# Gathering relation rows ahead of time: fewer groups in the first pass, more in the later layers, two tiles a bucket gathered on the spot

## The chip, the cores and the metric

The kernel runs on one core of one Trainium2 chip. The metric is the device time of one execution in microseconds (us); lower is better. The core has these engines, each with an instruction queue of its own that is worked off in order: PE (TensorE, matrix products), DVE (VectorE), ACT (ScalarE), POOL (GpSimd) and SP (SyncE, which here issues most of the transfers). Sixteen DMA engines move the data for all of them.

## The reference, cut to what matters

Four blocks follow each other over 3125 nodes of 256 features, and 103125 edges. Each adds its result to the nodes.

```python
x = x + _L0_gnn_ref(_layernorm(x), edge_index, ...)     # three graph layers
x = x + _L0_ffn_ref(_layernorm(x)[None], ...)[0]        # mixture of 16 experts, top 2
x = x + _L1_gnn_ref(_layernorm(x), edge_index, edge_type_500, ...)   # Clifford layer
x = x + _L1_ffn_ref(_layernorm(x)[None], ...)[0]        # mixture of 8 experts, top 2
```

The graph layers average the neighbours of each node (`segment_sum(h[src], dst) / deg`), multiply by two weight matrices, normalise, and add. The Clifford layer needs, for every edge, the source node's row times a row that belongs to the edge's relation, one of 500:

```python
h_src = h_hc[src]
r_uv = r_hc[edge_type]
m = clifford_linear(h_src * r_uv, msg_w, msg_b)
gate = sigmoid(r_uv.reshape(r_uv.shape[0], -1) @ gate_w.T + gate_b)
m = m * gate[:, :, None]                  # and times a norm by the degrees
h_agg = segment_sum(m, dst, num_segments=num_nodes)
h_out = clifford_linear(h_hc + h_agg, upd_w, upd_b)
```

Here only the rows of relations matter: 500 rows of 256 features and the gate, 257 numbers (`W`), multiplied by the gate beforehand and stored in the DRAM table `r_rows`.

## The kernel before, in words

The nodes are tiled into 25 buckets of 128 (`NB`, `P`). The edges of one target bucket are sorted in the first pass into 26 main tiles of 128 edges (`NS`, by source bucket) and 9 spill tiles (`SP`) for what doesn't fit.

**Stages.** (1) *First pass*: for each bucket `load` fetches windows of the edge list (`win`, SP), `rank` and `permute` place each edge in its tile (mostly DVE, with PE for counting), `lay` writes the tile's relation numbers to `main_t` and its sources to `main_s`, `build` makes the count matrix `cell` of the bucket and stores it in `cells`, and `sums_of` and `finish` compute the first graph layer. Four iterations overlap: bucket i is ranked while i-1 is permuted, i-2 is built and i-3 is summed. (2) *Layer 2* and (3) *layer 3*: `spread` prepares the rows of all buckets, then for each bucket the `cell` block is loaded again (SP, L834, four buffers, issued two iterations ahead), PE sums 75 products into `z`, and `finish` updates the nodes. In layer 2 DVE also reduces each `cell` block to degrees (`some_src`, L852) and works out the places of the spilled edges (`places`); in layer 3 the spill tiles are packed (`pack`) and the experts chosen (`choose`). (4) *The first mixture of experts* (`moe`): a routing part, then 34 tiles of 256 tokens whose rows POOL gathers (`xt`, L249, eight buffers) and whose results it scatters with addition (`f_total`, L1148). (5) *The Clifford buckets*: for every main tile PE picks the source rows with one-hot matrices (`hg_ps`, L1402), DVE multiplies them by the relation rows (`prod`, L1405), and PE sums by target with a second one-hot (`ps`, L1414). For spill tiles POOL gathers both factors itself (`hg`, `rg`, L249, six buffers each). (6) The second mixture of experts.

**Relation rows.** Main tiles don't gather their relation rows in the Clifford stage. They are gathered ahead, in groups of three tiles (`RG`): `fetch_relations(n, after)` takes the next n groups. For each it writes the relation numbers to `paced` with a small DVE operation (L296) that also reads the tile `after`, which ties the group to that point of the program; POOL then gathers three times 128 rows (L300) into `rel_rows` (four buffers). The store of a group to its DRAM tile `r_seq` (SP, L311) is issued when the next group is fetched. In the Clifford stage `relation(m)` loads two groups at a time back from `r_seq` (SP, L1376). Before the change the 650 main tiles make 217 groups that run across bucket borders.

**Who fetches.** In the first pass there are four calls of one group an iteration: at the end of `rank`, after `lay`, before `build` and after `finish`. In layer 2 `places` and `finish` call for one each; in layer 3 `choose` and `finish`. Ten more are asked for ahead of the first mixture of experts, and the rest after it. The order within each engine's queue isn't the program's: a scheduler orders the instructions of all stages by their dependences and its own idea of the times. By its order, all groups that were left stood on POOL ahead of the first token gather, or just after it.

**Order on SP.** In layers 2 and 3 the loads of `cell` blocks and the stores of `r_seq` are in one queue, two stores ahead of most loads. On DVE the reduction of block k (L852) stands ahead of the two fetches of bucket k-3. In the first pass one iteration's order on SP is three stores of groups, the store of a `cell` block, two window loads, one more store of a group, and the store of `main_s`.

Of the kernel before, what the change touches and what calls it, by code (L numbers as in the profile page):

```python
# [40 lines left out]
I32 = mybir.dt.int32  # L41
# [7 lines left out]
P = 128  # L49
N = 3125  # L50
NB = 25
# [11 lines left out]
NS = NB + 1  # L63
SP = 9
# [15 lines left out]
def gnn_moe_kernel(  # L80
# [177 lines left out]
    NM = NB * NS  # L258
    of_group = [range(t, min(t + RG, NM)) for t in range(0, NM, RG)]
# [24 lines left out]
    paced = rel_ctx.enter_context(tc.tile_pool(name="paced", bufs=1)).tile([P, NM], I32, name="paced")  # L284
# [37 lines left out]
    with ExitStack() as block:  # L322
# [65 lines left out]
        with ExitStack() as first:  # L388
# [256 lines left out]
            for i in range(NB + 3):  # L645
# [3 lines left out]
                if 0 <= i - 1 < NB:  # L649
                    moved[i - 1] = permute(i - 1, loaded.pop(i - 1), *ranked.pop(i - 1))  # L650
                    lay(i - 1, moved[i - 1])
                    if i > 1:
                        fetch_relations(1, words_of(moved[i - 1]))
# [4 lines left out]
                if 0 <= i - 3 < NB:  # L658
                    z = sums_of(i - 3, built.pop(i - 3), 0, psum)
                    done = finish(i - 3, z, 0)  # L660
                    if i > 3:
                        fetch_relations(1, done.bitcast(I32))
# [88 lines left out]
        with ExitStack() as later:  # L751
# [96 lines left out]
            for b, cell in enumerate(ahead_of(load_cell, 2)):  # L848
# [6 lines left out]
                fetch_relations(1, done.bitcast(I32))  # L855
# [19 lines left out]
            for b, cell in enumerate(ahead_of(load_cell, 2)):  # L875
# [5 lines left out]
                fetch_relations(1, done.bitcast(I32))  # L881
# [310 lines left out]
    with ExitStack() as block:  # L1192
# [107 lines left out]
        with ExitStack() as run:  # L1300
# [47 lines left out]
            DG = 7  # L1348
# [22 lines left out]
            def relation(m):  # L1371
                if m % (RC * RG) == 0:
                    held[0] = work.tile([P, RC, RG, W], F32, name="rg_seq", bufs=4)
                    first_g = m // RG
                    for i, g in enumerate(of_group[first_g:first_g + RC]):
                        nc.sync.dma_start(  # L1376
                            held[0][:, i, :len(g), :].rearrange("p r w -> p (r w)"),
                            r_seq[first_g + i])
                return held[0][:, m // RG % RC, m % RG, :]

            def summands():


                for b in range(NB):
                    s_oh = picks(b)

                    order = sorted([((t + 0.5) / NS, 0, t) for t in range(NS)] +
                                   [((t + 0.4) / SP, 1, t) for t in range(SP)])
                    d_oh = {}
                    for n, (_, spilled, t) in enumerate(order):  # L1390
                        ids = spill_d[:, b, :] if spilled else main_d[:, b, :]
                        if t % DG == 0:
                            d_oh[spilled] = drops(ids[:, t:min(t + DG, ids.shape[1])])
# [4 lines left out]
                        else:  # L1398
# [5 lines left out]
                            rg = relation(b * NS + t)  # L1404
                        nc.vector.tensor_mul(prod, hg, rg)  # L1405
                        yield (b, prod, d_oh[spilled][:, t % DG, :], n == 0,
# [74 lines left out]
```

## Time and profile before

| | |
|---|---|
| median of 3 runs | 3085.66 us (3076.42 to 3097.18) |
| the profiled execution | 3081.72 us, its span 3079.8 us |
| busy share of the span | PE 81%, weight load 64%, DVE 57%, ACT 14%, POOL 51% |
| granted PE clock, mean | 0.91 |
| relation gathers (L300) | 650, 761.3 us busy, 1.171 us each |
| first pass (130 to 706 us) | DVE 441.5 us busy, PE 404.4, POOL 381.0 |
| sums of layer 2 (771 to 1031 us) | PE 221.6 us busy, POOL 135.4, DVE 127.1 |
| sums of layer 3 (1087 to 1347 us) | PE 242.7 us busy, POOL 168.8, DVE 164.9 |
| Clifford buckets (1836 to 2565 us) | PE 700.6 us busy, DVE 577.9, POOL 466.3 |

The stage borders are read from the instructions in order of time. A busy time is that of an engine's instructions alone: the instruction that issues a transfer is short, the transfer itself is not in it. "A <- B" in a list of waits means that A stood still until B was done. The profiled execution's own time is its span and 1.9 us around it.

### The profile page before, as it was taken

To read this page: it belongs to the slowest core of one execution; us is meant where nothing else is said; L and a number is where in the kernel's file an instruction comes from. 1 tells how busy PE (TensorE), PEld (TensorE's weight loads), DVE (VectorE), ACT (ScalarE), POOL (GpSimd) and SP (SyncE) were. 2 spreads that over 40 slices of the span, in tenths; PEclk is the share of its full clock that TensorE was granted. 3 is DMA by queue.
4 is the path that set the end of the run, shared out by engine and by line. 5 is a ranking of instruction groups with operands and counts; after the bars stand their busy time and mean duration, and the time that the engine had idled before them with its cause. 6 is when DMAs were issued, how large, how long until landed. Compare 5 with 4: busy or idle time off the path is not lost.

```text
span 3079.8 us, 47955 instructions
## 1 busy us (share of the span) xinstructions
PE 2499.6 (81%) x17712; PEld 1986.2 (64%) x17712; DVE 1767.9 (57%) x4734; ACT 434.1 (14%) x1119; POOL 1566.1 (51%) x1379
## 2 busy tenths in 40 slices
PE   1767766778888999942999518999999996899997
PEld 0356654654777588832788406777777775788886
DVE  6688886766455366662233377788888787111110
ACT  1321221223000210000111050000000000122221
POOL 1067776761455256675566316666666660333331
PEclk9888897789999999976999859999999997899998
DMA  7046665652666368865777537777777770665653
GB/s 222 3 143 190 182 185 175 185 187 81 203 220 226 123 217 276 265 192 159 207 200 194 118 136 261 241 244 248 249 249 251 240 221 19 220 184 175 187 172 96
DMA packets 294160, 581.12 MB, mean 189 GB/s; under 512 B 77946, under 2 KB 176955, under 8 KB 289939
## 3 DMA queue, kind: packets, MB, share of 16 engines
q1 hardware_dynamic: 207459, 389.64, 36.9%
q0 software_dynamic: 76992, 177.86, 23.3%
q10 hardware_dynamic: 9456, 10.36, 1.1%
q8 instruction: 146, 2.39, 0.3%
q14 instruction: 107, 0.88, 0.1%
HBM read 433.05 MB, written 151.13 MB: 190 GB/s over the span
## 4 chain that ended last, share of the span: by engine, by line
PE 59%; DVE 15%; issue 7%; DMA 6%; another core or an unknown queue 5%; POOL 4%; ACT 1%; SPq 1%; POOLq 0%; DVEq 0%; ACTq 0%
PE ps L1414 12%; PE ph L1125 10%; PE py L1143 10%; PE hg_ps L1402 7%; PE z L362 5%; PE g L344 4%; POOL rel_rows L300 4%; PE z L359 2%; DVE oh_end L507 2%; DVE upto L539 2%; DMA cell<-cells 1%; PE pq L1043 1%; DMA rel_rows<-r_rows,paced 1%; DVE oh_slot L507 1%
## 5 line engine op out<-in xcount | busy, mean ns | idle before, releaser
L300 POOL DMA_INDIRECT rel_rows<-r_rows,paced x650 | 761.3, 1171 | 678.8 <-issue 158.6
L362 PE MATMUL z<-part_hi,cell 128*128 128x256 bf16 x3750 | 691.0, 285 | 23.9 <-issue 23.3
L359 PE MATMUL z<-part_lo,cell 128*128 128x256 bf16 (+1 forms) x1875 | 534.8, 285 | 18.4 <-issue 12.4
L1414 PE MATMUL ps<-prod,d_oh 128*128 128x257 f32 x1750 | 521.1, 392 | 26.5 <-issue 12.6
L362 PEld LDWEIGHTS <-cell 128*128 128x128 bf16 x3750 | 374.9, 102 | 85.0 <-issue 31.2
L1402 PE MATMUL hg_ps<-hc_part,s_oh 128*128 128x257 bf16 x1950 | 328.5, 275 | 98.0 <-DMA rg_seq<-r_seq 98.0
L1148 POOL DMA_INDIRECT f_total<-y,tok_s x126 | 198.3, 1574 | 354.0 <-DVE y L1146 275.3
L249 POOL DMA_INDIRECT hg<-hc_rows,spill_s x225 | 235.0, 1045 | 263.0 <-issue 125.9
L1143 PE MATMUL py<-w_t,hid 128*128 128x256 f32 x1472 | 335.1, 382 | 3.4 <-ACT hid L1134 3.4
L1125 PE MATMUL ph<-xT,w_t 128*128 128x256 f32 x1472 | 336.9, 386 | 0.8
L1405 DVE TENSOR_TENSOR prod<-hg_ps,rg_seq 128x257 f32<-128x257 f32 x650 | 270.4, 421 | 108.2 <-PE hg_ps L1402 65.2
L1414 PEld LDWEIGHTS ps<-prod,d_oh 128*128 128x128 f32 x1750 | 275.2, 191 | 81.5 <-issue 31.3
L1402 PEld LDWEIGHTS <-s_oh 128*128 128x128 bf16 x1950 | 191.6, 99 | 195.7 <-DVE s_oh L1358 98.4
L1146 DVE TENSOR_SCALAR y<-py,wt_q 128x256 f32<-128x256 f32 x126 | 61.0, 484 | 445.5 <-PE py L1143 440.8
L1125 PEld LDWEIGHTS ph<-xT,w_t 128*128 128x128 f32 x1472 | 280.4, 193 | 44.4 <-DVE xT L1115 3.7
L1143 PEld LDWEIGHTS py<-w_t,hid 128*128 128x128 f32 x1472 | 274.1, 191 | 50.8 <-ACT hid L1134 3.8
L249 POOL DMA_INDIRECT rg<-r_rows,spill_t x225 | 235.3, 1046 | 68.6 <-issue 68.6
L359 PEld LDWEIGHTS <-cell 128*128 128x128 bf16 x1875 | 192.5, 103 | 56.5 <-issue 23.1
L1134 ACT ACTIVATE hid<-ph,b_t 128x256 f32<-128x256 f32 x300 | 129.7, 471 | 647.8 <-PE ph L1125 524.8
L249 POOL DMA_INDIRECT xt<-f_x,tok_g x126 | 123.9, 983 | 99.0 <-DVE wt_q L1055 44.7
L507 DVE TENSOR_TENSOR oh_end<-held,iota 128x1024 bf16<-128x1024 f16 (+3 forms) x150 | 150.4, 1017 | 9.4 <-remote 5.0
L344 PE MATMUL g<-ww,hT 128*128 128x512 f32 x300 | 145.3, 629 | 8.2 <-ACT hT L143 8.0
(296 smaller groups left out, 2783.6 us busy)
## 6 DMA issues: line engine op xcount, KB each, us to landing
r_seq<-rel_rows SPq DMA_DIRECT2D x216, 385.5 KB
rg_seq<-r_seq SPq DMA_DIRECT2D x216, 385.5 KB
w_t<-in_L_ffn_W_dram SPq DMA_DIRECT2D x58, 1024.0 KB
cell<-cells SPq DMA_DIRECT2D x50, 800.0 KB
w_t<-in_L_ffn_w_dram SPq DMA_DIRECT2D x68, 512.0 KB
s_row<-main_s SPq DMA_DIRECT2D x25, 832.0 KB
cells<-cell SPq DMA_DIRECT2D x25, 800.0 KB
rel_rows<-r_rows,paced POOLq DMA_INDIRECT x650
```

The costliest lines, as they stand in the source:

```text
L249: nc.gpsimd.indirect_dma_start(out=rows, out_offset=None, in_=table, in_offset=bass.IndirectOffsetOnAxis(ap=ids, axis=0))
L300: nc.gpsimd.indirect_dma_start(out=rows[:, j, :], out_offset=None, in_=r_rows, in_offset=bass.IndirectOffsetOnAxis(ap=types[:, j:j + 1], a ...
L344: nc.tensor.matmul(g, hT[:, k, :], ww[:, layer, k, :], start=k == 0, stop=k == KD - 1)
L359: nc.tensor.matmul(z[:, :width], cell[:, sh, :], part_lo[:, sh, :width], start=sh == 0, stop=False)
L362: nc.tensor.matmul(z[:, :D], cell[:, sh, :], part_hi[:, sh, i, :], start=False, stop=sh == NB - 1 and i == 1)
L507: nc.vector.tensor_tensor(oh[:, :n, :, :], ids[:, :, None, :].to_broadcast([P, n, width, 2]), table[:, None, :width, :].to_broadcast([P, n ...
L1125: nc.tensor.matmul(ph[:, j - j0, :], w1_t[:, 0, k, j * P:(j + 1) * P], xT[:, k, :], start=k == 0, stop=k == KD - 1)
L1143: nc.tensor.matmul(py, hid[:, j, of], w2_t[:, 0, j, :], start=False, stop=j == nj - 1)
L1148: st = nc.gpsimd.indirect_dma_start(out=total, in_=y, in_offset=None, out_offset=bass.IndirectOffsetOnAxis(ap=tok_s[:, q:q + 1], axis=0), ...
L1402: nc.tensor.matmul(hg, s_oh[:, t, :], part[:, sh, i, :W], start=i == 2, stop=i == 0)
L1405: nc.vector.tensor_mul(prod, hg, rg)
L1414: nc.tensor.matmul(ps[b], d_oh, prod, start=is_first, stop=is_last)
```

## The change

It changes how many groups there are and where they are fetched. (1) The groups no longer cross bucket borders: 8 groups of three cover main tiles 0 to 23 of each bucket (`NK`), 200 groups in all. Main tiles 24 and 25 of a bucket are gathered in the Clifford stage from `r_rows`, by POOL, through the same six `rg` buffers as the spill tiles. (2) In the first pass two of the four calls are dropped: the one after `lay` and the one after `finish`. (3) In layers 2 and 3 the call after `finish` asks for two groups in odd buckets instead of one. (4) In a Clifford bucket the order of the 35 products is new: the 11 tiles that are gathered (9 spill, 2 main) are spread evenly among the 24 that are loaded. The one-hot tiles for the targets hold up to 8 columns instead of 7 for main tiles, and 5 and 4 for spill tiles.

```diff
-    NM = NB * NS
-    of_group = [range(t, min(t + RG, NM)) for t in range(0, NM, RG)]
+    NK = (NS - 2) // RG
+    of_group = [range(t, t + RG) for b in range(NB) for t in range(b * NS, b * NS + NK * RG, RG)]
...
                     lay(i - 1, moved[i - 1])
-                    if i > 1:
-                        fetch_relations(1, words_of(moved[i - 1]))
...
-                    done = finish(i - 3, z, 0)
-                    if i > 3:
-                        fetch_relations(1, done.bitcast(I32))
+                    finish(i - 3, z, 0)
...
                 done = finish(b, z, 1)
-                fetch_relations(1, done.bitcast(I32))
+                fetch_relations(1 + b % 2, done.bitcast(I32))
...
                 done = finish(b, z, 2)
-                fetch_relations(1, done.bitcast(I32))
+                fetch_relations(1 + b % 2, done.bitcast(I32))
...
-            DG = 7
+            DG = 8
...
-            def relation(m):
-                if m % (RC * RG) == 0:
+            def relation(b, t):
+                if t >= NK * RG:
+                    return gather(work, r_rows, W, main_t[:, b * NS + t:b * NS + t + 1], "rg", 6)
+                if t % (RC * RG) == 0:
                     held[0] = work.tile([P, RC, RG, W], F32, name="rg_seq", bufs=4)
...
-                    order = sorted([((t + 0.5) / NS, 0, t) for t in range(NS)] +
-                                   [((t + 0.4) / SP, 1, t) for t in range(SP)])
+                    loaded = NK * RG
+                    gathered = [(1, t) for t in range(SP)]
+                    for t in range(loaded, NS):
+                        gathered.insert((t - loaded + 1) * SP // (NS - loaded + 1) + t - loaded,
+                                        (0, t))
+                    order = sorted(
+                        [((t + 0.5) / loaded, 0, t) for t in range(loaded)] +
+                        [((i + 0.4) / len(gathered), *g) for i, g in enumerate(gathered)])
...
-                        if t % DG == 0:
-                            d_oh[spilled] = drops(ids[:, t:min(t + DG, ids.shape[1])])
+                        n_of = (DG, (SP + 1) // 2)[spilled]
+                        key = spilled, t // n_of
+                        if key not in d_oh:
+                            at = t // n_of * n_of
+                            d_oh[key] = drops(ids[:, at:min(at + n_of, ids.shape[1])])
```

More of the change, by code (lines that the diff above doesn't have):

```diff
@@ L283, in gnn_moe_kernel @@
     rel_ctx = ctx.enter_context(ExitStack())
-    paced = rel_ctx.enter_context(tc.tile_pool(name="paced", bufs=1)).tile([P, NM], I32, name="paced")
+    paced = rel_ctx.enter_context(tc.tile_pool(name="paced", bufs=1)).tile(
+        [P, NB * NS], I32, name="paced")
     stage = rel_ctx.enter_context(tc.tile_pool(name="rel_stage", bufs=4))
@@ L1369, in drops @@
                 return d_oh
-            def relation(m):
-                if m % (RC * RG) == 0:
+            def relation(b, t):
+                if t >= NK * RG:
+                    return gather(work, r_rows, W, main_t[:, b * NS + t:b * NS + t + 1], "rg", 6)
+                if t % (RC * RG) == 0:
                     held[0] = work.tile([P, RC, RG, W], F32, name="rg_seq", bufs=4)
[L1374 to L1379, printed above, removed]
+                    for i in range(RC):
+                        nc.sync.dma_start(held[0][:, i, :, :].rearrange("p r w -> p (r w)"),
+                                          r_seq[b * NK + t // RG + i])
+                return held[0][:, t // RG % RC, t % RG, :]
             def summands():
@@ L1403, in summands @@
                                                  start=i == 2, stop=i == 0)
-                            rg = relation(b * NS + t)
+                            rg = relation(b, t)
                         nc.vector.tensor_mul(prod, hg, rg)
-                        yield (b, prod, d_oh[spilled][:, t % DG, :], n == 0,
+                        yield (b, prod, d_oh[key][:, t % n_of, :], n == 0,
                                n == len(order) - 1)
```

## The prediction, made before the changed kernel had run

> **What bounds the kernel now.** I read the stage table first (busy time of each engine in stretches cut at the stage borders), then the waits of each stage, then the chain of waits inside one stage, then single instructions in order of time. The relation gathers (POOL L300, 650 of them, three to a group) run beside four stages, so each stage has to be judged by itself.
>
> Stretches: first pass, layer 2 sums, layer 3 sums, the gap before the first MoE, that MoE, the Clifford buckets. Columns: stretch, length, then busy time (and count) of PE, weight load, DVE, ACT, POOL, and the granted clock, the DMA share, GB/s.
>
> ```profile
> 130.00:706.00 576.00, 404.43 (x4953) 325.84 (x4952) 441.50 (x975) 111.66 (x278) 381.03 (x285) 0.84 0.57 169
> ...
> 771.00:1031.00 260.00, 221.55 (x1866) 183.51 (x1865) 127.05 (x323) 1.20 (x4) 135.40 (x143) 0.92 0.68 220
> ...
> 1087.00:1347.00 260.00, 242.72 (x2622) 208.42 (x2620) 164.91 (x691) 18.99 (x54) 168.77 (x151) 0.99 0.79 254
> ...
> 1421.00:1473.00 52.00, 8.29 (x24) 5.84 (x24) 0.76 (x2) 0.00 (x0) 35.09 (x37) 0.57 0.79 225
> 1473.00:1721.00 248.00, 246.67 (x1187) 208.86 (x1188) 82.95 (x190) 30.35 (x64) 151.32 (x118) 0.99 0.78 198
> ...
> 1836.00:2565.00 729.00, 700.61 (x4138) 533.31 (x4138) 577.87 (x1457) 40.37 (x121) 466.31 (x448) 0.98 0.74 240
> ```
>
> The reader is to see: DVE leads in the first pass (77%), no engine is full in layer 2 (PE 85%), PE sets layer 3 (93%), the MoE (99%) and the Clifford stage (96%). Between 1421 and 1473 nobody computes: the first expert tile waits for its token rows, which stand behind relation gathers on POOL.
>
> In layer 2 the waits of DVE name the transfer that nobody is supposed to wait for, and the chain between 925 and 960 us shows the ring behind it:
>
> ```profile
> DVE some_src L852 <- DMA cell<-cells: 77.6, 18, 9.8
> ```
>
> ```profile
> 925.27 4.41 DMA cell<-cells
> 929.67 1.72 issue
> 931.39 3.49 DVE some_src L852
> ...
> 942.96 3.63 DMA rel_rows<-r_rows,paced
> 947.15 4.89 DMA cell<-cells
> 952.93 3.49 DVE some_src L852
> ```
>
> Load of a cell block, DVE's reduction of it (in order ahead of the two fetches of the bucket three back), six gathers, their landing, the stores on SP, and only then the load of the block two further on: 947.15 - 925.27 = 21.9 us for two buckets. PE alone needs 221.6/25 = 8.9 us a bucket.
>
> **What the Trainium skill says.** "Perfetto Trace Analysis", Summary: the profiler window per engine type: the window of a POOL-issued DMA ends with its descriptors, the movement is hidden. The trace agrees: 0.95 us on POOL, but 3.63 us from the last gather's start to its landing. "SBUF — State Buffer", SBUF: two separate sides: while DVE runs certain two-port operations, POOL can't write descriptors. The trace agrees in its pattern: gathers last 0.943 to 3.072 us, mean 381.03/285 = 1.34 in the first pass, 0.95 in layer 2 and 1.13 in layer 3. "TensorE: Matmul & The Clock Gate", Part 1: an idle window of some 3.4 us halves the clock; here the clock is 0.84, 0.92 and 0.99 in the three passes, in the order of PE's idleness.
>
> **The change part by part.**
>
> *Where the groups go.* Before: 217 groups (95 in the first pass, 50 in layer 2, 50 in layer 3, 22 after). After: 25 buckets x 8 groups = 200 of which the first pass takes 23 + 24 = 47, layers 2 and 3 take 25 + 25 + 12 = 62 each, leaving 29. In the compiled order of POOL the stretch before the first token gathers holds 70 relation gathers in both kernels, and 23 more fall among the first expert tiles in the changed one.
>
> *First pass, what goes.* 48 groups, that is 144 gathers x (1.34 + 0.30 us between two) = 236 us of POOL, 48 stores on SP and 48 small DVE operations. It is tempting to book the 236 us; but the chain of the pass touches POOL and its transfers once only (444 to 465 us), and DVE is the one to ask. (1) 48 DVE operations at about 0.08 us from start to start: 4 us. (2) DVE waits for the window loads, which sit on SP behind stores that wait for gathers: 10.6 us in four waits, 4.5 us in one more at 185.75: 15 us. (3) The end of the pass: a branch waits for the last gathers, 701.3 to 706.8 us in the chain; the last group is now fetched a bucket earlier: 4 us. (4) Longer bubbles with PE and ACT (5.67, 5.84, 12.17, 3.87, 6.74, 4.95 us): sum 39, cause not visible in the trace; a few may come from a PE gone cold, since 490 to 500 us shows a clock of 0.5. Bounds 0 and 39; I take 10. Sum: -33 us, with -20 and -65 as ends. What is late next is DVE itself: quiet buckets already pass at 20.6 us with only some 3 us of waiting.
>
> *Layer 2, what is added.* Every odd bucket fetches three groups instead of two. In the compiled order of SP the load of an even-numbered block (from the eighth on) stands behind all three stores of the odd bucket that used to have two, and the reduction still stands ahead of the fetches on DVE. So the ring gains three gathers: 3 x (0.95 + 0.30) = 3.75 us. The other ring, of the odd blocks, is as before, but both go through the same in-order DVE and POOL, so the slower sets the pace: 21.6 + 3.75 = 25.4 us for two buckets, POOL being busy 15 x 1.25 = 18.8 of them. Nine turns of the ring: +34 us. Ends: +26 (a turn or two hidden) and +50 (PE, now idle up to 36% of the time, goes cold as in the first pass).
>
> *Layer 3.* Here the loads have room: block 24 is gated by the fetch of bucket 19, four buckets earlier, in both orders. PE's 10.3 us a bucket stay. But POOL needs 15 x (1.13 + 0.30) = 21.4 us for two buckets of 20.6: it falls behind by 0.8 us each time, some 10 us at the end. It used to wait there for its releasers by 27.9 + 22.9 us, which the 36 new gathers (51 us) eat. The lag costs nothing in the layer; it is paid in the gap before the MoE, where 70 gathers, and on SP 34 loads of expert numbers, stand in a row as before. +8 us (0 to 15). DMA share goes from 0.79 to about 0.9 by bytes; the four-buckets' room hides it.
>
> *First MoE.* 23 gathers x 1.25 = 29 us of POOL, ahead of some scatters. Token rows for five and a half tiles are gathered first and a tile takes 248/34 = 7.3 us; counting POOL's queue through, the rows of the seventh tile are gathered 42 us after the start and needed at 51. +1 us (0 to 8).
>
> *Clifford buckets.* 50 gathers more: POOL's mean there is 1.045 us, so 20 x 1.345 = 26.9 us of a bucket's 29.2, six buffers ahead. PE's work is the same, the one-hot tiles hold the same columns in the same six operations a bucket (8, 8, 8, 2 and 5, 4 for 7, 7, 7, 5 and 7, 2), and 17 fewer loads on SP. 0 us (-5 to +12).
>
> *Sum.* -33 + 34 + 8 + 1 + 0 = +10 us against this execution's 3081.7 (its span of 3079.8 and 1.9 around it): 3092. The median of the runs shown, 3085.7, stands 4 us above the profiled one, so this is between 3092 and 3096 against it; I give 3092. It is no difference: a measurement of this kernel tells about 1% (31 us) from none.
>
> **The rivals.**
> *Slower: POOL falls behind in layer 3.* If odd buckets catch DVE's long operations as the first pass does, a gather costs 1.34 + 0.30 = 1.64 us, 15 of them 24.6 us against 20.6, 4 us lost each pair, some 45 at the end of the layer, all of it paid in the gap before the MoE: 3092 - 8 + 45 = 3129. It decides from a mean pitch of 20.6/15 = 1.37 us on. For it: 1.43 today. Against: POOL waited 51 us in the layer and only part of DVE's work blocks it.
> *Faster: the first pass was paced by POOL after all.* Buckets that passed at 17.4, 18.5 and 19.0 us exist (from one scan L539 to the next); if the mean fell from 22.4 to 19, the pass gives 25 x 3.4 + 4 = 89 instead of 33: 3092 - 56 = 3036. For it: POOL's 12 gathers a bucket take 12 x 1.64 = 19.7 of 22.4 us. Against: DVE is busy 17 us a bucket and its short waits on PE recur without any transfer.
> *The ring of layer 2 doesn't stretch,* since something else already fills those 3.75 us: 3092 - 34 = 3058, just short of a gain that could be told. Against: the chain from gather to load has no slack in it.
>
> **How the numbers follow.** Forecast, within its own 3055 to 3116: 0.43, with the third rival inside it. POOL behind in layer 3, or a colder PE in layer 2 with it: 0.30. First pass paced by POOL: 0.27. So faster by over 1% 0.27, within 1% 0.43, slower by over 1% 0.30. Range 3033 to 3132: to the two outer rivals, with a tenth left beyond each.
>
> **What would show it.** Right: layer 2's cell loads come in pairs 25 us apart (21.9 now), DVE's wait for them grows by some 35 us, the first pass shortens by 20 to 65 us with DVE at 80% or more, POOL waits for almost nothing in layer 3, and the gap before the MoE is 50 to 65 us. Wrong: a pair pitch under 23 us, a first pass shorter by over 70 us, a gap over 75 us, or PE idle in the Clifford stage for token or relation rows.

## The result, and the profile after

The changed kernel takes 3201.25 us (median of 4 runs, 3182.09 to 3215.37) against 3084.05 us for the kernel before (4 runs beside it): ratio 1.037, 95% interval 1.0295 to 1.0448. It is slower; the forecast was 3092 us. The profiled execution took 3213.51 us, its span is 3211.6.

The stretches of the changed kernel, cut where the same stage begins and ends in it: first pass, layer 2, layer 3 (from its first product, so its counterpart of before is 302 us, not the 260 us that begin after the last block of the spread), first mixture, Clifford buckets. Columns as ahead: stretch, length, busy time (and count) of PE, weight load, DVE, ACT, POOL, granted clock, DMA share, GB/s.

```profile
129.00:585.00 456.00, 358.86 (x4961) 295.51 (x4959) 433.34 (x932) 107.12 (x279) 240.75 (x144) 0.95 0.45 133
644.00:969.00 325.00, 247.70 (x1873) 191.58 (x1871) 130.31 (x339) 1.58 (x5) 169.94 (x180) 0.82 0.66 204
978.00:1342.00 364.00, 318.92 (x2768) 237.34 (x2766) 187.21 (x740) 40.35 (x117) 196.12 (x179) 0.94 0.64 205
1470.00:1766.00 296.00, 272.82 (x1274) 227.87 (x1274) 87.19 (x200) 32.24 (x68) 182.36 (x148) 0.95 0.75 192
1869.00:2693.00 824.00, 729.61 (x4127) 550.05 (x4128) 575.90 (x1453) 40.90 (x120) 515.87 (x499) 0.95 0.67 213
```

The reader is to see: DVE fills 95% of the first pass (433.34 of 456), PE no longer fills layer 3 or the Clifford stage, and PE's granted clock is down to 0.82 in layer 2. With the same borders in both profiles (the first or last PE instruction of a stage), the difference of the spans, 131.9 us, is made up so:

| stage | before | after | difference |
|---|---|---|---|
| first pass | 580.0 | 455.8 | -124.2 |
| layer 2 | 261.1 | 325.0 | +63.9 |
| layer 3 | 302.2 | 364.1 | +61.9 |
| from layer 3 to the first mixture | 127.2 | 128.7 | +1.5 |
| first mixture | 270.4 | 294.4 | +24.0 |
| Clifford stage | 725.2 | 824.8 | +99.6 |
| all else | 813.7 | 818.8 | +5.1 |

Up to the end of layer 3 the gain and the losses almost cancel (+1.6 us), so that the loss is about that of the mixture and the Clifford stage.

Layer 2 of the changed kernel, on SP and on DVE, in order of time (start, length, engine and line, how many in a row; in brackets the wait before it):

```profile
838.38 0.32 SPq L831 DMA_DIRECT2D cell<-cells  x1
838.98 8.55 SPq L312 DMA_DIRECT2D r_seq<-rel_rows  x2
847.63 0.36 SPq L831 DMA_DIRECT2D cell<-cells  x1
854.18 7.95 SPq L312 DMA_DIRECT2D r_seq<-rel_rows  x3
865.93 0.32 SPq L831 DMA_DIRECT2D cell<-cells  x1
```

```profile
843.79 3.49 DVE L849 TENSOR_REDUCE some_src<-cell 128x25 f32<-128x3200 bf16 x1 [4.38 <-DMA cell<-cells]
852.40 3.49 DVE L849 TENSOR_REDUCE some_src<-cell 128x25 f32<-128x3200 bf16 x1 [2.65 <-DMA cell<-cells]
865.94 0.48 DVE L376 SCALAR_TENSOR_TENSOR zt<-z,inv_dst,own 128x256 f32<-128x256 f32 x1 [8.57 <-remote]
870.99 3.49 DVE L849 TENSOR_REDUCE some_src<-cell 128x25 f32<-128x3200 bf16 x1 [4.04 <-DMA cell<-cells]
```

The loads alternate: two stores and a load, three stores and a load. Two blocks take 865.93 - 838.38 = 27.6 us; it was 21.9, and 25.4 was predicted. But the three stores don't end the wait of the last load here: SP is done with them at 854.18 + 7.95 = 862.13 us and issues the load at 865.93, just when DVE, after 8.57 us, can read PE's sums `z`. The lists of waits of the stage (who waited for what: us in total, times, longest) say the same. "issue" stands where an engine waited for nothing that the profile shows, "remote" where the profile knows no source. These names have a limit: this profile and that of the kernel before record only some 40% of the landings of transfers (in the Clifford stage 4731 where 12,624 are due), so that a wait for a landing can go under another name. That an engine stood still, and for how long, does not depend on it:

```profile
DVE zt L376 <- remote: 90.2, 11, 13.4
DVE some_src L849 <- DMA cell<-cells: 64.9, 18, 6.2
PE z L363 <- issue: 52.7, 66, 1.8
PE z L360 <- issue: 19.8, 26, 1.8
```

DVE's wait for the loads of cell blocks did not grow: it was 77.6 us before. DVE waits for `z` instead (1.5 us under this name before), and PE stands for 72.5 us between the products of its blocks without any wait (28.5 us before). In layer 3 PE does so too; first the changed kernel, then the kernel before:

```profile
PE z L363 <- issue: 23.3, 43, 1.1
PE z L360 <- issue: 12.0, 25, 1.1
```

```profile
PE z L362 <- issue: 1.0, 2, 0.8
PE z L359 <- issue: 0.8, 1, 0.8
```

The waits in the Clifford stage of the changed kernel:

```profile
DVE prod L1411 <- PE hg_ps L1408: 110.0, 187, 2.4
PE ps L1420 <- issue: 49.2, 40, 5.3
PE ps L1420 <- DVE prod L1411: 39.1, 34, 3.3
POOL rg L249 <- DVE prod L1411: 172.8, 112, 3.5
```

DVE and PE wait for each other, and POOL has time to spare: it waits for products that free its buffers. In the kernel before the first was 65.2 us, PE's two 12.6 and 10.7. Nothing in these lines names what began it. Of the 99.6 us more, some 32 are PE's own work: it was busy for 729.61 us, in the kernel before within the same borders (1836 to 2561 us) for 697.84, with the same products, at a granted clock of 0.95 instead of 0.98. The other 68 are time in which PE stood still.

### The profile page after: what moved, and what is told of

Same layout as the page of the kernel before. It is cut to its first block, busy times and chain, and to the rows that moved or that the text cites. A ratio compares the mean times of both kernels' runs of the same rounds, so it can differ in the third digit from the quotient of the medians.

```text
span 3211.6 us, 47915 instructions
## 1 busy us (share of the span) xinstructions
PE 2540.9 (79%) x17712; PEld 1987.6 (62%) x17712; DVE 1759.8 (55%) x4717; ACT 430.4 (13%) x1119; POOL 1563.1 (49%) x1379
## 5 line engine op out<-in xcount | busy, mean ns | idle before, releaser
L301 POOL DMA_INDIRECT rel_rows<-r_rows,paced x600 | 708.9, 1181 | 755.2 <-DVE paced L297 162.0
L1420 PEld LDWEIGHTS ps<-prod,d_oh 128*128 128x128 f32 x1750 | 287.8, 196 | 155.4 <-issue 72.6
L1140 PE MATMUL py<-w_t,hid 128*128 128x256 f32 x1472 | 337.5, 383 | 17.1 <-issue 10.7
L1411 DVE TENSOR_TENSOR prod<-hg_ps,rg_seq 128x257 f32<-128x257 f32 x600 | 250.1, 421 | 173.1 <-PE hg_ps L1408 100.1
L249 POOL DMA_INDIRECT rg<-r_rows,spill_t x225 | 244.5, 1087 | 171.9 <-DVE prod L1411 126.1
L1140 PEld LDWEIGHTS py<-w_t,hid 128*128 128x128 f32 x1472 | 274.7, 192 | 66.5 <-issue 13.6
L249 POOL DMA_INDIRECT hg<-hc_rows,spill_s x225 | 226.1, 1005 | 156.1 <-issue 155.8
L249 POOL DMA_INDIRECT xt<-f_x,tok_g x126 | 123.7, 982 | 99.6 <-DVE wt_q L1052 44.8
```

The source lines that it names most:

```text
L249: nc.gpsimd.indirect_dma_start(out=rows, out_offset=None, in_=table, in_offset=bass.IndirectOffsetOnAxis(ap=ids, axis=0))
L301: nc.gpsimd.indirect_dma_start(out=rows[:, j, :], out_offset=None, in_=r_rows, in_offset=bass.IndirectOffsetOnAxis(ap=types[:, j:j + 1], a ...
L1140: nc.tensor.matmul(py, hid[:, j, of], w2_t[:, 0, j, :], start=False, stop=j == nj - 1)
L1420: nc.tensor.matmul(ps[b], d_oh, prod, start=is_first, stop=is_last)
```

## The experiments

They ran on several chips, beside the kernel before on the same chip each time. On one chip the kernel before takes 3091 us, about as in the result above, whose chip isn't on record; on four others 2950 to 2960. The runs are told by that number, "the slower chip" and "the faster chips", and ratios are within a chip. Each chip was used at one time only, so that the chip and the hour can't be told apart. b_again and b_third are one execution each. Stage times come from the profile of one execution, with the borders of the table above:

| run | groups by end of layer 3 | first pass | layer 2 | layer 3 | first mixture | Clifford | median, ratio |
|---|---|---|---|---|---|---|---|
| *slower chip* | | | | | | | |
| b_again (before) | 195 | 581 | 265 | 302 | 272 | 728 | 3089, - |
| a_again (after) | 171 | 456 | 327 | 370 | 297 | 841 | 3214, 1.040 |
| e5_layers_one | 147 | 458 | 270 | 302 | 385 | 836 | 3192, 1.035 |
| e6_three | 183 | 519 | 261 | 365 | 264 | 828 | 3169, 1.027 |
| *faster chips* | | | | | | | |
| b_third (before) | 195 | 542 | 252 | 281 | 264 | 685 | 2965, - |
| a_third (after) | 171 | 455 | 297 | 302 | 273 | 709 | 2982, 1.012 |
| e1_clifford_alone | 195 | 521 | 254 | 281 | 263 | 703 | 2931, 0.990 |
| e2_no_gather | 171 | 455 | 298 | 297 | 284 | 680 | 2965, 1.002 |
| e3_old_order | 171 | 457 | 301 | 300 | 284 | 682 | 2972, 1.004 |
| e4_store_act | 171 | 571 | 254 | 387 | 264 | 706 | 3146, 1.063 |
| e7_own_old_order | 195 | 537 | 246 | 281 | 264 | 681 | 2904, 0.983 |
| e8_store_pool | see text | 457 | 200 | 282 | 299 | 681 | 3051, 1.034 |
| e9_own_bufs | 195 | 531 | 251 | 281 | 264 | 708 | 2926, 0.993 |
| e10_own_no_gather | 195 | 532 | 257 | 281 | 264 | 680 | 2901, 0.984 |
| e13_own_by_gathers | 195 | 543 | 253 | 281 | 264 | 699 | 2924, 0.989 |
| e14_act_layer2 | 195 | 532 | 216 | 281 | 264 | 698 | 2882, 0.977 |
| e15_own_nine | 195 | 541 | 257 | 281 | 264 | 708 | 2926, 0.991 |
| e16_old_order_act | 195 | 533 | 211 | 281 | 264 | 681 | 2866, 0.972 |

### The parts one by one

**e1_clifford_alone**: the changed kernel with the fetches of before.

```diff
                     lay(i - 1, moved[i - 1])
+                    if i > 1:
+                        fetch_relations(1, words_of(moved[i - 1]))
...
-                    finish(i - 3, z, 0)
+                    done = finish(i - 3, z, 0)
+                    if i > 3:
+                        fetch_relations(1, done.bitcast(I32))
...
-                fetch_relations(1 + b % 2, done.bitcast(I32))
+                fetch_relations(1, done.bitcast(I32))
```

> The changed kernel with the fetches of before: four groups an iteration in the first pass, one per call in layers 2 and 3 (195 of the 200 groups are fetched by the end of layer 3, 5 are left for the first mixture of experts). The Clifford part of the change alone. In the trace of the changed kernel the Clifford stage lasts 824 us instead of 724. Theory A (the Clifford part costs by itself): Clifford stage 810 to 830 us, first pass and layers as before, about 5 us less ahead of the first mixture; 3165 to 3190 us. Rival B (the Clifford stage is slowed by what the fetches left behind, or by chance of place): Clifford stage 720 to 740, total 3070 to 3090 us.

Measured: ratio 0.990 (0.9882 to 0.9919), Clifford stage 703 us. This ran on a faster chip, so neither sum fits as it stands. The Clifford stage there is 18 us longer than before's 685 (b_third, on another of the faster chips), and the shorter way from layer 3 to the mixture (5 groups left instead of 22) more than pays for that: 78 us against 123.

**e2_no_gather** and **e3_old_order**: each takes one half of the Clifford part away.

```diff
-                    return gather(work, r_rows, W, main_t[:, b * NS + t:b * NS + t + 1], "rg", 6)
+                    return held[0][:, t % RC, t % RG, :]
```

> The changed kernel, but main tiles 24 and 25 of a bucket aren't gathered: their product reads relation rows of a group that was loaded for other tiles (left out: 50 gathers of 128 rows). Order of the products and one-hot tiles as in the changed kernel. Theory A1 (the 50 gathers in the Clifford stage cost the 100 us, 2 us each): Clifford stage 720 to 740 us, total 3095 to 3115 us. Rival A2 (the new order of products and one-hot tiles costs it): Clifford stage stays at 800 to 825, total 3185 to 3205 us.

```diff
-                    order = sorted(
-                        [((t + 0.5) / loaded, 0, t) for t in range(loaded)] +
-                        [((i + 0.4) / len(gathered), *g) for i, g in enumerate(gathered)])
+                    order = sorted([((t + 0.5) / NS, 0, t) for t in range(NS)] +
+                                   [((t + 0.4) / SP, 1, t) for t in range(SP)])
```

> The changed kernel with the order of products of before (26 main tiles and 9 spill tiles spread each by itself), so that main tiles 24 and 25, still gathered in the Clifford stage, come last in their bucket. Theory A1 (the 50 gathers cost): Clifford stage stays at 800 to 830 us, total 3185 to 3215. Rival A2 (the order costs): Clifford stage 720 to 745 us, total 3095 to 3120 us.

Measured: Clifford stage 680 and 682 us, ratios 1.002 (1.0007 to 1.0033) and 1.004 (1.0021 to 1.0048). Neither theory: on a faster chip the gathers alone cost nothing, and the order alone costs nothing; both together do (703 us in e1 on the same chip).

**b_again** and **a_again**: the two kernels themselves.

> The kernel before, unchanged, for its stages on the chip on which the experiments run (the first four were run beside a median of 2960.25 us for the kernel before, 4% below the 3084 us at which the change was measured). Either the difference is in all stages alike (clock), or in those that gather or load most: Clifford stage then 680 to 705 us instead of 725, first pass 520 to 540 instead of 580, the second mixture 445 us as it was.

> The changed kernel, unchanged, on this chip. Theory A (the Clifford part as a whole, gathers in this order, costs on any chip): Clifford stage 790 to 830 us, ratio to before 1.03 to 1.045. Rival C (the order and the gathers by themselves cost nothing; the 100 us came from the state of the transfers on the chip of the first measurement): Clifford stage 680 to 705 us as in the two runs with the order or the gathers undone, ratio 1.00 to 1.01, with the gain of the first pass given back in layers 2 and 3 alone.

Both ran on the slower chip. Measured for a_again: 1.040 (1.0321 to 1.048), Clifford stage 841 us against 728: theory A, a little above its 790 to 830. The result repeats there stage by stage: -125.3, +61.8, +67.7, +25.4, +112.3 us for first pass, layers 2 and 3, mixture, Clifford stage.

### What a group costs, and where

**e5_layers_one**: one group per call in layers 2 and 3. **e6_three**: three calls in the first pass, and one group per call in layer 2 only.

```diff
-                fetch_relations(1 + b % 2, done.bitcast(I32))
+                fetch_relations(1, done.bitcast(I32))
```

> The changed kernel with one group per call in layers 2 and 3, as before the change; so 147 groups are fetched by the end of layer 3, and 53 are left for the first mixture. The first-pass part alone, with its groups put after layer 3. Theory R (the added fetches stretch the ring of layers 2 and 3): layer 2 back to 250 to 262 us from 300, layer 3 to 281 to 290 from 298; but the time from the end of layer 3 to the Clifford stage longer by 24 groups of 3 gathers at 1.26 us, 91 us, less what hides under the mixture's products: 40 to 90 us. Ratio to before 0.99 to 1.01. Rival P (layers 2 and 3 are slowed by the order on SP that the scheduler chose, not by the number of gathers): layer 2 stays at 290 to 300; ratio 1.02 to 1.04.

```diff
                     lay(i - 1, moved[i - 1])
+                    if i > 1:
+                        fetch_relations(1, words_of(moved[i - 1]))
...
-                fetch_relations(1 + b % 2, done.bitcast(I32))
+                fetch_relations(1, done.bitcast(I32))
```

(The second edit is made in layer 2 alone.)

> The changed kernel with three calls an iteration in the first pass (the one after the laying out restored: 71 groups), one group per call in layer 2 (50), one and two by turns in layer 3 (62): 183 groups by the end of layer 3, 17 left. If the first pass is paced by POOL's gathers and their transfers, it lies half way between 455 us (two calls) and the time with four: 480 to 495 us. Layer 2 as with one group per call, 250 to 260 us; layer 3 285 to 300. Ratio to before 0.975 to 0.99. Rival: with three calls the first pass is as long as with four (the third gather group is what exceeds POOL's turn): 515 us and ratio 0.99 to 1.0.

Stretches of e5 (layer 3, first mixture), then of e6 (first pass, layer 3, first mixture):

```profile
921.00:1222.00 301.00, 290.44 (x2766) 231.52 (x2766) 187.14 (x749) 39.88 (x115) 162.43 (x143) 1.00 0.68 216
1353.00:1738.00 385.00, 288.99 (x1276) 237.54 (x1275) 87.94 (x201) 32.25 (x68) 249.68 (x218) 0.85 0.75 194
```

```profile
128.00:647.00 519.00, 383.09 (x4961) 311.96 (x4959) 439.65 (x957) 110.82 (x279) 317.11 (x214) 0.88 0.52 153
974.00:1339.00 365.00, 322.45 (x2775) 242.63 (x2774) 186.34 (x729) 40.44 (x117) 195.85 (x179) 0.92 0.65 205
1452.00:1716.00 264.00, 263.05 (x1267) 222.82 (x1268) 87.04 (x199) 31.71 (x67) 158.87 (x124) 0.99 0.79 195
```

e5: 1.035 (1.0272 to 1.0422), layers back to 270 and 302 us, as theory R said; the ratio was missed, since the groups moved into the mixture cost it 385 - 297 = 88 us and the Clifford stage stayed long. e6: 1.027 (1.019 to 1.0344); its first pass, 519 us, lies half way between 456 and 581, as the theory said. In numbers it was a miss: 480 to 495 us for the first pass, 285 to 300 for layer 3 (365 measured) and a ratio of 0.975 to 0.99 were expected, from times of a faster chip.

With the four runs of one chip the price of a group can be read stage by stage:

- first pass: 456, 519, 581 us with 47, 71, 95 groups: 62.5/24 = 2.6 us a group.
- layer 2: 261 to 270 us with 50 (e6, b_again, e5), 327 with 62: 4.8 to 5.5 us a group.
- layer 3: 302 us with 50 (b_again and e5), 365 to 370 with 62 (e6, a_again): 5.2 to 5.7 us.
- first mixture: 264 us with 17 left, 272 with 22, 297 with 29, 385 with 53: 1.6, 3.6 and 3.7 us a group.

On this chip the change moved groups from where they cost 2.6 us to where they cost 3.6 to 5.7. On the faster chips the prices are lower and stand in another order: from b_third to a_third 87/48 = 1.8 us a group in the first pass, 45/12 = 3.7 in layer 2, 21/12 = 1.7 in layer 3 and 9/7 = 1.3 in the mixture. There only layer 2 is dearer than the first pass.

### Whether stores on SP make the ring

**e4_store_act**: all stores of groups from ACT.

```diff
-        nc.sync.dma_start(r_seq[i], rows[:, :n, :].rearrange("p r w -> p (r w)"))
+        nc.scalar.dma_start(r_seq[i], rows[:, :n, :].rearrange("p r w -> p (r w)"))
```

> The changed kernel with the stores of relation groups issued by ACT instead of SP, so that loads of count blocks in layers 2 and 3 and of weights in the first mixture no longer stand behind stores that wait for gathers. Theory R (the ring over SP's queue sets layers 2 and 3): two buckets of layer 2 take 20 to 22.5 us instead of 27.4, two of layer 3 about 20.6 instead of 23.9, the first mixture 20 us less; total 3050 to 3085 us. Rival P (POOL's gathers or the transfers themselves are too many for these layers): pairs stay at 25 to 28 us in layer 2, total 3170 to 3205 us. ACT may be held by the stores, which would show as PE or DVE waiting for ACT.

Measured: 1.063 (1.0603 to 1.0653). Layer 2 fell to 254 us with all its 62 groups, from 297 to 301 (theory R). The mixture took 264 us, but that is no gain: all 94 gathers that were left ran ahead of it, and the time from layer 3 to the mixture grew to 143 us from 128 in a_third. First pass and layer 3, where ACT has its own work, grew to 571 and 387 us (in layer 3 PE waited 64.9 us for ACT's `rT`), so the whole is slower, and the 3050 to 3085 us of theory R were missed.

**e8_store_pool**: stores from the 48th group on issued by POOL, with the order of products of before.

```diff
-        nc.sync.dma_start(r_seq[i], rows[:, :n, :].rearrange("p r w -> p (r w)"))
+        queue = nc.gpsimd if i >= 47 else nc.sync
+        queue.dma_start(r_seq[i], rows[:, :n, :].rearrange("p r w -> p (r w)"))
```

> The changed kernel with two edits: the stores of all groups from the 48th on are issued by POOL instead of SP, and the order of products is that of before. SP's loads of count blocks then stand behind no store. Theory R (the ring over SP's queue stretches layers 2 and 3): layer 2 in 255 to 270 us instead of 325, layer 3 in 300 to 315 instead of 364 to 370 (250 and 281 on the faster chip, from 300), with 62 groups in each as in the changed kernel; total of about 2985 to 3010 us if the old order restores the Clifford stage. Rival P (12 more groups cost what POOL and the transfers need for them): layers stay at 320 and 360. POOL issues 153 stores more, about 1 us each, in stages where it is idle half the time.

Measured: 1.034 (1.0317 to 1.0366), a miss. Layers 2 and 3 took 200 and 282 us, but only 102 and 135 gathers fell into them (172 and 179 in e3_old_order); 216 came after layer 3, 156 of them beside the routing, which stretched from 71 (a_third) to 265 us. The layers were short because POOL did less there: this run doesn't show what holds layer 3.

**e14_act_layer2**: only the stores of layer 2 from ACT (with the fetches of before and the order of e13, below).

```diff
-        nc.sync.dma_start(r_seq[i], rows[:, :n, :].rearrange("p r w -> p (r w)"))
+        queue = nc.scalar if 97 <= i < 144 else nc.sync
+        queue.dma_start(r_seq[i], rows[:, :n, :].rearrange("p r w -> p (r w)"))
```

> As the one before, and the stores of the groups fetched in layer 2 are issued by ACT. Theory R: without the stores ahead of its loads layer 2 is paced by POOL's turn, 144 gathers at 1.3 to 1.4 us, or by PE: 195 to 215 us instead of 250 (265); the rest unchanged, ratio to before 0.96 to 0.97. Rival: ACT, held by the wait for a gather, holds the evictions of layer 2, and the stage stays at 250 to 265 us.

Measured: 0.977 (0.9744 to 0.9788), layer 2 216 us instead of 253 with as many gathers in it (145; 140 in e13). Theory R holds for layer 2 on a faster chip; its range, 195 to 215 us, was missed by a little.

### Why the Clifford stage waits

**e7_own_old_order**: e1 with the order of products of before (the edit of e3).

> The fetches of before (four an iteration, one per call: 195 groups early), tiles 24 and 25 gathered in the Clifford stage, but the order of products of before, so that the two come last in their bucket. On the chip where the kernel before takes 3090 us the Clifford stage of the changed kernel takes 825 to 841 us, on the other one 703. Theory O (the new order, together with the gathers, makes the stage wait): Clifford stage 720 to 740 us here (680 on the faster chip), total 3075 to 3095 (2905 to 2915). Rival G (the 50 more gathers fill POOL's turn: 20 gathers at 1.3 us are 26 us of a bucket's 28): Clifford stage 800 to 840 whatever the order, total 3170 to 3190 us.

Measured, on a faster chip: 0.983 (0.9791 to 0.987), Clifford stage 681 us: theory O there, and G is out there, since it has all 50 gathers.

**e10_own_no_gather**: e1 without the gathers (the edit of e2).

> The fetches of before and the Clifford part of the change in its new order, but tiles 24 and 25 of a bucket use relation rows loaded for other tiles (left out: 50 gathers). Theory G (the gathers): Clifford stage 720 to 735 us (680 on the faster chip). Rival N (the new order and the one-hot tiles by themselves): 800 to 830 us. Total 3065 to 3085 us or 3150 to 3180 us (2905 on the faster chip).

Measured: 0.984 (0.9804 to 0.9883), 680 us: the order without the gathers costs nothing, as in e2.

**e9_own_bufs** and **e15_own_nine**: e1 with more buffers.

```diff
-                    return gather(work, r_rows, W, main_t[:, b * NS + t:b * NS + t + 1], "rg", 6)
+                    return gather(work, r_rows, W, main_t[:, b * NS + t:b * NS + t + 1], "rg", 11)
...
-                    held[0] = work.tile([P, RC, RG, W], F32, name="rg_seq", bufs=4)
+                    held[0] = work.tile([P, RC, RG, W], F32, name="rg_seq", bufs=3)
...
-                            rg = gather(work, r_rows, W, spill_t[:, b, t:t + 1], "rg", 6)
+                            rg = gather(work, r_rows, W, spill_t[:, b, t:t + 1], "rg", 11)
```

> The fetches of before, the Clifford part of the change as it is (new order), but 11 buffers instead of 6 for gathered relation rows, and three instead of four for loaded ones. If the two tiles that share the six buffers take POOL's lead away (6 buffers hold 9 spill tiles' rows for two thirds of a bucket, 11 tiles' for half), the Clifford stage falls to 730 to 760 us (690 on the faster chip). If the buffers are not what it waits for: 820 to 840 us (703).

(e15 has 9 for `rg` and 9 for `hg`, whose number was 6, and 3 for `rg_seq`.)

> The fetches of before and the order of the change, with nine buffers instead of six for each of the two kinds of gathered rows in the Clifford stage (three instead of four for loaded relation rows). With 11 buffers for relation rows alone the stage took 708 us instead of 703, and the wait moved from relation rows to source rows. If the lead of POOL is what lacks at the border of two buckets, nine of each hold a whole bucket's spill tiles: 680 to 690 us (730 to 745 where the kernel before takes 3090). If POOL's turn is simply full: 700 to 708 (825 to 840).

Measured: 0.993 (0.9903 to 0.9956) and 0.991 (0.9884 to 0.9934), Clifford stage 708 us in both. Buffers are not it.

**e13_own_by_gathers**: the gathered tiles spread by the number of their gathers.

```diff
-                        [((i + 0.4) / len(gathered), *g) for i, g in enumerate(gathered)])
+                        [((sum(1 + spilled for spilled, _ in gathered[:i]) + 0.8) /
+                          (SP + len(gathered)), *g) for i, g in enumerate(gathered)])
```

> The kernel before, unchanged, for its Clifford stage beside that of the next three. If the machine is one on which it takes 3090 us: 725 to 730 us, as twice measured. If it is one on which it takes 2950 to 2960: theory G' (the part of the change costs there too, POOL's turn being full) 678 to 685 us, as with the order or the gathers undone; rival: 700 to 710, so that the part costs nothing there.

> The fetches of before, two tiles gathered in the Clifford stage, and the gathered tiles spread evenly by the number of their gathers (two for a spill tile, one for a main tile) instead of by their number. Theory G' (nine spill tiles at steps of 1/11 of a bucket ask POOL for two gathers in 2.6 us, which its 1.3 to 1.4 us a gather can't give; it falls behind from the sixth spill tile of a bucket to the third of the next, which stand without a main tile between them): Clifford stage 678 to 690 us where the kernel before takes 2955, 725 to 745 where it takes 3090. Rival M (any gather of a main tile amid the bucket costs, as it holds one of three PSUM tiles until it has landed): as with the even order, 703 and 825 to 840 us.

Measured: b_third 685 us; e13 0.989 (0.9857 to 0.9927), 699 us: theory G' got the stage of before right, but its remedy recovered only some 5 of the 18 to 24 us. The rival's 703 is nearer.

**e16_old_order_act** puts the two repairs together: e7 and the stores of e14. **a_third** is the changed kernel.

> The version that the runs point to: the fetches of before (four an iteration in the first pass, one per call in layers 2 and 3), 200 groups with two tiles of a bucket gathered in the Clifford stage but last in their bucket (order of products of before), and the stores of the groups fetched in layer 2 issued by ACT. Layer 2 200 to 216 us, Clifford stage 678 to 685 us where the kernel before takes 2955: 2850 to 2870 us, ratio 0.965 to 0.972. Where it takes 3090: with theory O (the order makes the stage wait there too) Clifford stage 720 to 740 us, total 3010 to 3035; with rival G (50 more gathers cost there in any order) 800 to 840 us, total 3110 to 3140.

> The changed kernel, unchanged. Where the kernel before takes 2955: from the runs so far first pass 456, layer 2 300, layer 3 298, time from layer 3 to the first mixture's end 415, Clifford stage 700 to 710, so 2985 to 3000 us and ratio 1.01 to 1.015. Where it takes 3090: 3190 to 3225 us, ratio 1.035 to 1.045, Clifford stage 825 to 841, as twice measured.

Both ran on a faster chip. Measured: e16 0.972 (0.9696 to 0.9739), 2866 us, faster than both kernels; a_third 1.012 (1.009 to 1.0151), within what was expected. On that chip the change costs 24 us in the Clifford stage, not 100.

What bounds the stage there can be read from stretches and waits. First a_third, then b_third, e13 and e7:

```profile
1753.00:2463.00 710.00, 689.49 (x4132) 538.08 (x4132) 571.01 (x1455) 40.82 (x120) 550.32 (x499) 0.98 0.78 247
DVE prod L1411 <- DMA rg<-r_rows,spill_t: 37.0, 23, 4.1
POOL hg L249 <- issue: 58.5, 192, 0.3
POOL rg L249 <- DVE prod L1411: 31.1, 102, 0.3
```

```profile
1761.00:2446.00 685.00, 682.66 (x4132) 533.12 (x4132) 575.67 (x1454) 39.93 (x120) 471.51 (x448) 0.99 0.78 256
POOL hg L249 <- DVE prod L1405: 94.0, 140, 2.2
```

```profile
1700.00:2400.00 700.00, 677.97 (x4091) 527.91 (x4092) 571.51 (x1451) 41.94 (x123) 544.40 (x500) 0.99 0.79 252
DVE prod L1416 <- DMA rg<-r_rows,spill_t: 39.8, 33, 3.1
```

```profile
1699.00:2380.00 681.00, 676.63 (x4132) 533.63 (x4130) 571.39 (x1453) 39.91 (x120) 505.26 (x497) 1.00 0.79 257
DVE prod L1414 <- DMA rg<-r_rows,spill_t: 5.7, 6, 1.7
```

In a_third POOL never stands still for more than the 0.3 us between two gathers: 499 x (550.32/499 + 0.30) = 700 us of the stage's 710. It is full, and DVE waits 37 us for rows of spill tiles. In b_third POOL still waited, up to 2.2 us at a time. In e7, with as many gathers in another order, a gather takes 505.26/497 = 1.02 us instead of 1.10, so 654 us in all with the 0.30 between two, and PE sets the stage again. So on the faster chips the 18 to 24 us are POOL's turn: a ninth more gathers, and each longer in the new order than in e7's. Why a gather is then longer, no run shows.

On the slower chip this is not the cause. There POOL stands waiting for DVE's products (172.8 us in the lines of the changed kernel above). The traces show this much: of the 278 products in a_again that waited after DVE's last operation, 81 began more than 1 us after the last matmul of their tile started; in b_again 33 of 183; in e1 and e7 0 of 191 and 1 of 223, where 0.31 us is the rule. And of 135 us that DVE spent in the changed kernel in pauses of over 0.9 us, 99 lie in the first 12 us after the issue of a bucket's `s_row` load, which are 36% of the stage; in the kernel before it is 26 of 52. What PE or its signal waits for there is not in the trace, and no run with the order or the gathers undone came to that chip. The 100 us stay unexplained, but for the 32 of PE's longer work.

## Why the prediction was wrong

**First pass: the step that failed is (4), the bubbles that were priced at 10 of 39 us, and with it the choice that "DVE is the one to ask".** -33 was predicted, with -20 to -65 as ends; -124 was measured, beyond even the rival's -89. The three sizes of e6 and the two kernels lie on a straight line of 2.6 us a group, which the list of named waits (15 us for windows, 4 for the end) doesn't contain: even at their upper bounds the four terms give 4 + 15 + 4 + 39 = 62 us. Only with 47 groups DVE fills the pass. The rival's sign was right: fetches did pace the pass. Whether through POOL, the stores on SP or the two engines' hindrance of each other isn't settled; the runs give the price, not the carrier.

**Layer 2: the step that failed is "the ring gains three gathers: 3 x (0.95 + 0.30) = 3.75 us".** +34 (26 to 50) was predicted and +64 measured. Had the ring stretched as told, DVE's wait for the cell loads would have grown by some 35 us; on this chip it fell from 77.6 to 64.9, and in its place came 90.2 us in which DVE waited for PE's `z`, while PE paused for 72.5 us instead of 28.5 with no wait to name. The sum had no term for that, and what makes PE pause stays open. In these pauses the transfers of gathers keep 6.5 of the 16 DMA engines busy on average, outside them 3.4; that they go together is all that this shows. On the faster chips the ring is as predicted in kind: the wait for the cell loads is 105.6 us in b_third and 147.1 in a_third (+42), PE has no such pause, and the layer grows by 45 us, within the ends of +26 and +50. There e4, e14 and e16 confirm the ring by breaking it: without the stores on SP 62 groups fit into 254 us and 50 into 211 to 216. PE's clock fell with its idleness, as the upper end had it: the Trainium skill ("TensorE: Matmul & The Clock Gate", Part 1) ties the clock to windows of some 3.4 us in which PE idles, and here it is 0.82 in place of 0.92.

**Layer 3: "PE's 10.3 us a bucket stay" and "The lag costs nothing in the layer" failed.** +8 (0 to 15) was predicted, +62 measured, and 365 to 370 against 302 us between runs that differ by these 12 groups. In the kernel before, the blocks after the first follow each other at 10.3 us with few exceptions; in the changed one most even blocks still do, and most odd ones take 13.6 to 18.0. Of the 62 us, some 33 are pauses of PE without a named wait (35.3 us, before 1.8; 2.1 in e5 and 30.7 in e6), and some 27 are PE's own work, 318.92 us instead of 292.04 for the same products, at a granted clock of 0.94 instead of 1.00. POOL did not fall behind, as the slower rival had it: the time from layer 3 to the mixture grew by 1.5 us only. That these groups lengthen the layer is shown by e5 and e6; what holds PE there is not, nor whether it has to do with the loads that were said to have room.

**First mixture: +1 (0 to 8) failed by size.** POOL's queue was counted to the seventh tile, and in that the step was right: PE waits 0.8 us for token rows.

```profile
PE py L1140 <- issue: 10.7, 3, 8.7
PE pt L1107 <- DMA xt<-f_x,tok_g: 0.8, 1, 0.8
```

It waits 22 us for other things, the longest of them not named (before: 4.5 us in all), and the stage grew by 24 us, and by 88 more with 24 groups more (e5). So groups left over aren't hidden there. What the step left out is SP: at 1494.78 us two stores of groups hold it for 9.08 us, and the next load of an expert's weights goes out behind them, at 1504.55. That PE waits for such a load fits, but no line names it.

**Clifford stage: 0 (-5 to +12) failed, and was the largest error together with the first pass.** The step is "20 x 1.345 = 26.9 us of a bucket's 29.2, six buffers ahead". On the faster chips the mean was 1.40, not 1.345, and PE needs only 27.3 us there, so that what seemed a reserve of 2.3 us a bucket was a lack of 0.7. On the slower chip 100 us came, 32 from PE's longer work and 68 from waits that the prediction had no step for. PE idle in the Clifford stage "for token or relation rows" was named as a sign of a wrong forecast. PE was idle, and on the faster chips DVE does wait for relation rows (37 us in a_third); the lists of the slower chip name no such wait.

Of the forecast's total, the first pass erred by -91 us and the other stages by +30, +54, +23 and +100: of five steps four had the right sign, none the right size. That the sum up to the end of layer 3 came out near the forecast, +1.6 against +9 us, is luck. The measured 3201 us lie above the range's 3132. The slower rival rested on POOL's lag paid in the gap, which didn't occur; only the colder PE in layer 2, named beside it, did.

## What to carry to other kernels

When work is moved between stages, measure the price of one unit in each stage before moving it, by a run with a few units fewer in each: here, on the slower chip, 2.6 us in the stage that looked crowded and about 5 in layers 2 and 3, of which layer 2 had no full engine. And measure it on the chip that counts: on the faster chips layer 3 took groups at 1.7 us. A load that must not be late doesn't belong behind stores that wait for gathers; moving only the stores of one stage to an engine idle in that stage gave 37 us, while with all of them moved the kernel was 6% slower than before. And POOL, which stood at 92% of its turn by mean durations, proved full: its gathers took 1.10 us instead of 1.05 when there were more of them.

## What was not expected of the hardware

The same program takes 2950 to 2965 us on some chips and 3084 to 3091 on others, and the difference isn't spread evenly: the second mixture takes 444 to 445 us on both and the first pass with two fetches 455 to 458, but the first pass with four 542 and 581, layer 3 281 and 302, the Clifford stage 685 and 728. An edit's price differs too: the whole change costs 1.2% on one and 4.0% on the other. The traces differ in kind as well. In all six profiles of the slower sort, that of the first measurement counted in, PE pauses between products of one block with no wait that the profile shows: 29 to 79 us in layer 2 and 1 to 35 us in layer 3. In the fourteen profiles of the faster chips there is not one such pause in these layers. Those six also record 37 to 45% of the landings in these layers and the Clifford stage, the fourteen 96% and more, so that causes found on the faster chips rest on fuller lists than those on the slower one; but pauses between products of one block, whatever their name, come to at most 9 us in layer 2 and none in layer 3 of the fourteen. Whether it is the chip or the hour isn't shown.
